# Eight of nine one-hot tiles of the weighted sums made on GpSimd, between the gathers

## The chip, the cores and the metric

The kernel runs on one core of a Trainium2 chip. The core has a matrix engine (TensorE, in the profile PE, with its weight loads PEld), two engines for elementwise work (VectorE or DVE, ScalarE or ACT), GpSimd (POOL), which here issues the indirect transfers that gather rows, and SyncE (SP), which issues the plain transfers. The metric is the device time of one execution in microseconds (us); lower is better.

## The reference

A graph layer over 12500 nodes with 128 features and 412500 edges sorted by destination. For each edge a gate is computed from the difference of the two end nodes, the gated differences are summed per destination, a dense term times the number of incoming edges is added, and the result, with the input added, is normalized per node.

```python
theta = x[dst] - x[src]
w = jax.nn.sigmoid(jax.nn.relu(theta @ W1 + b1) @ W2 + b2)
w_theta = w * theta
agg = jax.ops.segment_sum(w_theta, dst, num_segments=n_nodes)
indeg = jax.ops.segment_sum(jnp.ones((dst.shape[0], 1), x.dtype), dst, num_segments=n_nodes)
out = agg + indeg * (x @ W4 + b4)
x = layernorm(x + out)
```

(Here `n_nodes` is 12500, and the last two lines stand for the return value and the normalization around it.)

## The kernel before, in words

**Tables and edges.** A table `z` in device memory holds for each node 256 values: the 128 products with W1 and the 128 features themselves. The edges, in order of destination, are cut into *parts*. The first 26 parts (`PLAIN`) hold 1024 edges each and serve as a start while tables are built. After them come 234 *later parts* of up to 1656 edges each, numbered s = 26 to 259. Two parts are a block (`b`, `h = divmod(s, 2)`), and a block's results go to a window of 112 nodes (`WB`).

**Two kinds of edges in a later part.** 640 "hot" edges of a later part (`HK`, five tiles of 128) have source nodes that are taken by matrix products from a table kept in SBUF. The others are fetched by eight gathers (`gather`, L369; L380 in the profile), each of 128 rows of 256 values. The gathered tiles k and k+4 hold, row by row, two edges with the same destination, so that four (`J`) one-hot tiles serve all eight. GpSimd's queue holds gather after gather. Between every two stands an instruction that computes nothing that is used: in the later parts a memset of `rest_t`, 128 x 320 (L374). Each is tied by order to the instruction before it, so that the queue is gather, memset, gather, memset. The first gather of a part also waits for the newest TensorE product issued so far (`paced`): that is the pace. The gathers of part s+3 (`LEAD`) are issued in the code of part s.

**Work of a later part** (`part`, L1343), in the order of the code, which is also the order on TensorE, VectorE and ScalarE (their order is written out by hand; GpSimd's follows from the ties just told):
1. `logits`: VectorE subtracts, takes the maximum with zero, multiplies and adds up 1024 columns of gathered rows (L896, L898, L899).
2. `gather(s + 3)` on GpSimd.
3. `add_part(s - 1)`: TensorE sums the part before it (L1083). Each product has a one-hot tile as weights, which says for each of 128 edges to which of the 112 nodes it belongs. There are four one-hot tiles `ow` for the gathered rows and five `owh` for the hot edges, nine in all.
4. gates: `hot_logits` (L1054), `weigh` (L928), `hot_weights` (L1063 and the one-hot tiles `owh`, L1066), `gate_sums`, `one_hot_w` (the one-hot tiles `ow`, L873), the rest of the weighing on ScalarE (L919).
5. `products_ahead`: TensorE's products for the next part (L1025, L1029, L1021, L1040).
6. at the end of a block: its total (L1121, L1129) and normalization (L1156, L1162 and on).
7. `spend`: steps of the placing of the next edge lists (sorting out 64 parts at a time on VectorE: L547, L549, L552, L642 and others), as many as a credit per part allows.

Between steps 2 and 5 ScalarE and TensorE also fetch hot rows (L966, L968, L980).

**The one-hot tiles.** VectorE compares a row of numbers 0 to 111, copied to PSUM (`fix`, `iota_f`), with each edge's place (`rel` for gathered, `hrel` for hot edges, bfloat16). One instruction makes all four `ow` tiles (128 x 448), one makes all five `owh` tiles (128 x 560). They are made in the code of the part itself, and used by `add_part` in the code of the part after it. The buffers of `ow` are four deep and those of `owh` two.

Of the kernel before, what the change touches and what calls it, by code (L numbers as in the profile page):

```python
# [22 lines left out]
K = 8  # L23
# [57 lines left out]
def gnn_resnorm(  # L81
# [284 lines left out]
    table_steps = []  # L366
    paced = {}

    def gather(s):  # L369

        (src_i, _, _), i = set_of(s)
        for k in slots(s):
            if gathers:
                rest = nc.gpsimd.memset(rest_t, 0.0) if s >= NH else nc.gpsimd.engine_nop()  # L374
                tc.add_manual_dep(
                    rest.ins, gathers[-1].ins.name,
                    mybir.DependencyInfo(mybir.DependencyClass.NoSync, mybir.DependencyReason.DATA),
                    reason="between two gathers")
                gathers.append(rest)
# [9 lines left out]
            for other, kind in waits:  # L389
                tc.add_manual_dep(  # L390
                    ins.ins, other.ins.name,
                    mybir.DependencyInfo(kind, mybir.DependencyReason.DATA), reason="gathers' pace")
            gathers.append(ins)


    base_b = const.tile([1, NK], I32, name="base_b")
# [280 lines left out]
    with tc.manual_schedule(engines={SP}), tc.tile_pool(name="work", bufs=2) as wp, tc.tile_pool(  # L677
# [168 lines left out]
        def spread_y(s):  # L846
# [17 lines left out]
                                            y_of(s), start=s >= NH, stop=True, skip_group_check=s < NH)  # L864
            return last

        def one_hot_w(s):

            (_, rel, _), i = set_of(s)
            parts[s]["ow"] = []  # L870
            for k0 in range(0, K if s < PLAIN else J, J):
                ow = wp.tile([P, J, WB], F32, name="ow", bufs=4)
                nc.vector.tensor_tensor(  # L873
                    ow, iota_f.to_broadcast([P, J, WB]),
                    rel[:, k0:k0 + J, i:i + 1].to_broadcast([P, J, WB]), op=OP.is_equal)
                parts[s]["ow"].append(ow)
# [182 lines left out]
        def hot_weights(s):  # L1059

            wx = parts[s]["wxh"]
            for q in range(HQ):
                nc.scalar.activation(wx[:, q, :D], hot_x(s, q), AF.Copy, scale=wx[:, q, D:D + 1])  # L1063
            (_, hrel, _), j = hot_set(s)
            owh = parts[s]["owh"] = wp.tile([P, HQ, WB], F32, name="owh")
            nc.vector.tensor_tensor(  # L1066
                owh, iota_f.to_broadcast([P, HQ, WB]),
                hrel[:, j, :].rearrange("p (q o) -> p q o", o=1).to_broadcast([P, HQ, WB]), op=OP.is_equal)

        def shift(b):  # L1070

# [271 lines left out]
        def part(s):  # L1343
# [26 lines left out]
            if PLAIN + AHEAD <= s + LEAD < NS:  # L1370
                if s >= PLAIN + 4:
                    paced[s + LEAD] = newest[0]
                gather(s + LEAD)
            if PLAIN <= s - 1 < NS:
                add_part(s - 1)
            if now:
# [230 lines left out]
```

## Time and profile before

| | us |
|---|---|
| median of three runs | 3414.64 (3405.97 to 3415.9) |
| the profiled execution, own time | 3395.38 |
| its span | 3393.6 |
| TensorE busy | 2713.4 |
| VectorE busy | 2641.6 |
| ScalarE busy | 2363.5 |
| GpSimd busy | 2821.6 |

The rows quoted below are of four kinds. A *group* row has line, engine, operation, output and inputs, shape and count, then busy us, mean ns of one, and after the second bar the engine's idle us just before these instructions and what ended most of it ("issue" is time in which it waited for nothing that the profile shows). A row *in order of time* has the start and the duration in us, then the instruction; in brackets stands the idle time before it. A row of a *stretch* has its bounds and length, then busy us and count (x) of the instructions asked for or of PE, PEld, DVE, ACT and POOL, then the granted TensorE clock, the DMA share and GB/s. The *chain* gives shares of the span of the work that ended last, followed back from the last instruction.

### The profile page before, as it was taken

To read this page: it belongs to the slowest core of one execution; us is meant where nothing else is said; L and a number is where in the kernel's file an instruction comes from. 1 tells how busy PE (TensorE), PEld (TensorE's weight loads), DVE (VectorE), ACT (ScalarE), POOL (GpSimd) and SP (SyncE) were. 2 spreads that over 40 slices of the span, in tenths; PEclk is the share of its full clock that TensorE was granted. 3 is DMA by queue.
4 is the path that set the end of the run, shared out by engine and by line. 5 is a ranking of instruction groups with operands and counts; after the bars stand their busy time and mean duration, and the time that the engine had idled before them with its cause. 6 is when DMAs were issued, how large, how long until landed. Compare 5 with 4: busy or idle time off the path is not lost.

```text
span 3393.6 us, 62355 instructions
## 1 busy us (share of the span) xinstructions
PE 2713.4 (80%) x18615; PEld 2351.2 (69%) x18615; DVE 2641.6 (78%) x6197; ACT 2363.5 (70%) x5856; POOL 2821.6 (83%) x4093
## 2 busy tenths in 40 slices
PE   6776778787788787888788878888878888888887
PEld 5676767676677676777677766676667777677776
DVE  6797458898888689888888858888887866666666
ACT  4554567776677677777777767777767777777774
POOL 5678778888888888888888888888888888888883
PEclk9876678898899888999898889899988999998998
DMA  7564434444444444444444444444444444444441
GB/s 255 184 169 121 119 93 121 118 111 117 121 113 120 128 113 116 121 117 121 122 118 120 116 118 123 117 117 124 116 115 123 115 122 117 119 122 118 126 110 55
DMA packets 265060, 416.67 MB, mean 123 GB/s; under 512 B 66608, under 2 KB 178217, under 8 KB 264205
## 3 DMA queue, kind: packets, MB, share of 16 engines
q0 software_dynamic: 98528, 267.78, 28.5%
q1 hardware_dynamic: 164219, 138.42, 15.6%
q10 hardware_dynamic: 1970, 6.40, 0.5%
q8 instruction: 154, 2.52, 0.3%
q14 instruction: 189, 1.55, 0.2%
HBM read 384.89 MB, written 27.49 MB: 122 GB/s over the span
## 4 chain that ended last, share of the span: by engine, by line
DVE 30%; ACT 25%; PE 16%; issue 11%; POOL 8%; DMA 5%; another core or an unknown queue 4%; DVEq 0%; SPq 0%; POOLq 0%; ACTq 0%
POOL zbuf L380 6%; ACT wxh L1063 5%; PE pd L980 4%; DVE hh L1054 4%; DVE zbuf L896 4%; DVE zbuf L898 4%; ACT zbuf L919 4%; DVE lg L899 4%; ACT of L966 4%; PE pa L1083 4%; POOL rest_t L374 2%; DMA zbuf<-z,src_i 2%; ACT of L968 2%; DVE ed L549 2%
## 5 line engine op out<-in xcount | busy, mean ns | idle before, releaser
L380 POOL DMA_INDIRECT zbuf<-z,src_i x1866 | 1816.1, 973 | 421.0 <-issue 261.6
L980 PE MATMUL pd<-of,tabs 128*128 128x128 f32 (+4 forms) x4816 | 685.9, 298 | 181.6 <-ACT of L968 95.8
L374 POOL MEMSET rest_t<- 128x320 f32 x2010 | 800.4, 398 | 1.0
L980 PEld LDWEIGHTS pd<-of,tabs 128*128 128x128 f32 x4816 | 628.9, 209 | 224.7 <-ACT of L968 113.5
L1083 PE MATMUL pa<-zbuf,ow 128*112 128x260 f32 (+1 forms) x2282 | 588.1, 406 | 47.6 <-ACT zbuf L919 21.6
L1083 PEld LDWEIGHTS pa<-zbuf,ow 128*112 128x112 f32 x2282 | 407.4, 200 | 157.7 <-ACT zbuf L919 30.1
L1025 PE MATMUL pxa<-wni,xT 128*128 128x128 f32 x1872 | 303.8, 311 | 258.0 <-DVE hh L1054 241.5
L1025 PEld LDWEIGHTS pxa<-wni,xT 128*128 128x128 f32 x1872 | 266.1, 218 | 281.8 <-DVE hh L1054 261.0
L966 ACT ACTIVATE of<-hot_src,nodes 128x512 f32<-128x512 f16 (+3 forms) x602 | 394.1, 709 | 7.1 <-issue 4.3
L919 ACT ACTIVATE zbuf<-zbuf 128x128 f32<-128x128 f32 x1144 | 362.8, 389 | 0.4
L1040 PE MATMUL y<-y,oh 64*128 64x128 f32 x1872 | 341.1, 323 | 14.2 <-issue 14.0
L1029 PE MATMUL pxa<-y,oh 64*128 64x128 f32 x1872 | 336.9, 323 | 9.9 <-issue 9.6
L1054 DVE SCALAR_TENSOR_TENSOR hh<-pxa,w_r 128x128 f32<-128x128 f32 x936 | 270.7, 289 | 92.9 <-remote 48.2
L1083 PEld LDWEIGHTS pa<-wxh,owh 128*112 128x112 f32 x2340 | 295.2, 177 | 34.8 <-issue 12.6
L968 ACT ACTIVATE of<-of 128x1024 f32<-128x1024 f32 (+3 forms) x301 | 310.8, 1033 | 9.2
L1083 PE MATMUL pa<-wxh,owh 128*112 128x130 f32 x2340 | 308.9, 276 | 5.8 <-issue 4.4
L994 ACT ACTIVATE xT<-pd 128x512 f32<-128x512 f32 (+7 forms) x496 | 185.7, 416 | 183.2 <-PE pd L980 59.5
L1029 PEld LDWEIGHTS pxa<-y,oh 64*128 64x128 f32 x1872 | 275.2, 219 | 49.5 <-issue 26.9
L928 DVE TENSOR_TENSOR zbuf<-zbuf,fix 128x512 f32<-128x512 f32 x234 | 160.2, 684 | 186.4 <-ACT fix L903 118.9
L896 DVE TENSOR_TENSOR zbuf<-y,zbuf 128x1024 f32<-128x1024 f32 x234 | 285.5, 1220 | 13.5 <-issue 3.5
L898 DVE SCALAR_TENSOR_TENSOR zbuf<-zbuf,fix 128x1024 f32<-128x1024 f32 x234 | 285.7, 1221 | 8.0
L899 DVE TENSOR_REDUCE lg<-zbuf 128x8 f32<-128x1024 f32 x234 | 285.5, 1220 | 8.0
(265 smaller groups left out, 4710.0 us busy)
## 6 DMA issues: line engine op xcount, KB each, us to landing
to_all<-off_d SPq DMA_DIRECT2D x234, 144.0 KB
hot_src<-hot_s SPq DMA_DIRECT2D x257, 128.0 KB
zbuf<-z,src_i POOLq DMA_INDIRECT x1866
z<-zbuf SPq DMA_DIRECT2D x8, 1024.0 KB
xw<-in_x_dram SPq DMA_DIRECT2D x130, 56.0 KB
u<-u_d SPq DMA_DIRECT2D x130, 56.0 KB
out_dram<-o SPq DMA_DIRECT2D x130, 56.0 KB
y<-z SPq DMA_DIRECT2D x252, 28.0 KB
```

The lines of the kernel that those rows point to most:

```text
L374: rest = nc.gpsimd.memset(rest_t, 0.0) if s >= NH else nc.gpsimd.engine_nop()
L380: ins = nc.gpsimd.indirect_dma_start(out=rows_of(s)[:, k, :], out_offset=None, in_=z if s >= NH else x, in_offset=IndirectOffsetOnAxis(ap= ...
L896: nc.vector.tensor_sub(half, yy.to_broadcast([P, 2, J, D]), half)
L898: nc.vector.scalar_tensor_tensor(h, h, 0.0, w2.to_broadcast([P, K, D]), op0=OP.max, op1=OP.mult)
L899: nc.vector.tensor_reduce(lg[:, :, 0], h, AX.X, OP.add)
L919: nc.scalar.activation(wx[:, k, :D], wx[:, k, :D], AF.Copy, scale=wx[:, k, D:D + 1])
L966: nc.scalar.activation(of[:, t, :], hot_src[:, i % NU, :w], AF.Abs, bias=nodes[:, t:t + 1])
L980: newest[0] = nc.tensor.matmul(to[:, q], tabs[:, g * RG + q, t, :], of[:, t, q], start=t == 0, stop=t == HT - 1)
L1025: nc.tensor.matmul(hot_y(s, q), xT[:, q * P:(q + 1) * P], wneg, start=q % G == 0, stop=False, skip_group_check=True)
L1029: newest[0] = nc.tensor.matmul(hot_y(s, q), d["oh"][:, BP + q * P:BP + (q + 1) * P], y_of(s), start=False, stop=True, skip_group_check=True)
L1054: nc.vector.scalar_tensor_tensor(h, hot_y(s, q), 0.0, w2_r, op0=OP.max, op1=OP.mult, accum_out=lg[:, q, :])
L1083: newest[0] = nc.tensor.matmul(to if len(w.shape) == 3 else to[:, 0, :], one, w, start=first and i == 0, stop=last and i == len(terms) - 1)
```

## The change

The code of later part s now gives `gather(s + 3, ...)` a list of eight small instructions, which make on GpSimd the four `ow` tiles of part s+1 and the first four of its five `owh` tiles. Each is a tensor-scalar comparison of 128 x 112 in SBUF: the row of numbers, in SBUF now (`iota_row`), against one column of places. One of them goes in front of each gather, and the memset between it and the gather has 64 columns instead of 320. VectorE makes only the fifth `owh` tile (128 x 112). The buffers of `owh` become three deep. Parts 28 to 257 have their tiles from GpSimd; parts 26, 27, 258 and 259 have theirs from VectorE as before.

```diff
-    def gather(s):
+    def gather(s, between=()):
         (src_i, _, _), i = set_of(s)
+        between = list(between)
         for k in slots(s):
             if gathers:
-                rest = nc.gpsimd.memset(rest_t, 0.0) if s >= NH else nc.gpsimd.engine_nop()
+                rest = between.pop(0)() if between else None
+                if rest is not None:
+                    tc.add_manual_dep(
+                        rest.ins, gathers[-1].ins.name,
+                        mybir.DependencyInfo(mybir.DependencyClass.NoSync, mybir.DependencyReason.DATA),
+                        reason="between two gathers")
+                    gathers.append(rest)
+                    rest = nc.gpsimd.memset(rest_t[:, :64], 0.0)
+                else:
+                    rest = nc.gpsimd.memset(rest_t, 0.0) if s >= NH else nc.gpsimd.engine_nop()
...
             gathers.append(ins)
+        for fill in between:
+            fill()
...
+        made = {}
+
+        def one_hots_between(s):
+
+            (_, rel, _), i = set_of(s)
+            (_, hrel, _), j = hot_set(s)
+            ow = wp.tile([P, J, WB], F32, name="ow", bufs=4)
+            owh = wp.tile([P, HQ, WB], F32, name="owh", bufs=3)
+            made[s] = ow, owh
+            iota = iota_row[:, :WB]
+
+            def one(to, at):
+                return lambda: nc.gpsimd.tensor_scalar(to, iota, at, None, op0=OP.is_equal)
+
+            return ([one(ow[:, k, :], rel[:, k, i:i + 1]) for k in range(J)]
+                    + [one(owh[:, q, :], hrel[:, j, q:q + 1]) for q in range(K - J)])
+
         def one_hot_w(s):
 
             (_, rel, _), i = set_of(s)
+            if s in made:
+                parts[s]["ow"] = [made[s][0]]
+                return
...
-            owh = parts[s]["owh"] = wp.tile([P, HQ, WB], F32, name="owh")
+            owh, q0 = (made[s][1], K - J) if s in made else (wp.tile([P, HQ, WB], F32, name="owh", bufs=3), 0)
+            parts[s]["owh"] = owh
             nc.vector.tensor_tensor(
-                owh, iota_f.to_broadcast([P, HQ, WB]),
-                hrel[:, j, :].rearrange("p (q o) -> p q o", o=1).to_broadcast([P, HQ, WB]), op=OP.is_equal)
+                owh[:, q0:, :], iota_f.to_broadcast([P, HQ - q0, WB]),
+                hrel[:, j, q0:].rearrange("p (q o) -> p q o", o=1).to_broadcast([P, HQ - q0, WB]),
+                op=OP.is_equal)
...
-                gather(s + LEAD)
+                gather(s + LEAD, one_hots_between(s + 1))
```

## The prediction

> **What bounds the kernel now.** I read the page first (busy times, slices, shares of the chain), then GpSimd's groups of instructions, its order of time, and its stretches.
>
> The page, busy times and the shares of the chain that ended last:
>
> ```profile
> PE 2713.4 (80%) x18615; PEld 2351.2 (69%) x18615; DVE 2641.6 (78%) x6197; ACT 2363.5 (70%) x5856; POOL 2821.6 (83%) x4093
> DVE 30%; ACT 25%; PE 16%; issue 11%; POOL 8%; DMA 5%; another core or an unknown queue 4%; DVEq 0%; SPq 0%; POOLq 0%; ACTq 0%
> ```
>
> By the shares VectorE (DVE) looks like the bound and GpSimd (POOL), at 8%, like a bystander; taking 1 us a part off VectorE then looks like a gain. The groups say otherwise. GpSimd's groups between 600 and 3300 us of the span, a stretch of 2700 us in which only later parts run; then the memset's row by source (min/median/max ns), and three consecutive rows in order of time:
>
> ```profile
> L380 POOL DMA_INDIRECT zbuf<-z,src_i x1711 | 1665.9, 974 | 357.7 <-issue 238.6 <-PE pd L980 29.2 <-remote 23.4
> L374 POOL MEMSET rest_t<- 128x320 f32 x1710 | 680.2, 398 | 0.8
> ...
> L374 POOL MEMSET rest_t<- x1710: 378/379/976, 601.0 to 3299.2; 128x320 f32 x190
> ...
> 1538.38 0.95 POOL L380 DMA_INDIRECT zbuf<-z,src_i  x1 [0.17 <-issue]
> 1539.34 0.38 POOL L374 MEMSET rest_t<- 128x320 f32 x1
> 1539.88 0.95 POOL L380 DMA_INDIRECT zbuf<-z,src_i  x1 [0.17 <-issue]
> ```
>
> A gather, its memset and 0.17 us that precede every gather whatever else happens make 1.50 us. In the 2700 us, 1665.9 + 680.2 + 1711 x 0.17 = 2637 us are this cycle; real waits are the rest of the idle time, 357.7 - 1711 x 0.17 = 66.8 us, 39 ns a gather, 2.5%. GpSimd has practically no spare time. The gathers counted in three stretches show the same:
>
> ```profile
> 600.00:1400.00 800.00, 490.23 (x501) 0.90 0.44 118
> 1400.00:2700.00 1300.00, 803.71 (x823) 0.91 0.45 119
> 2700.00:3300.00 600.00, 371.30 (x388) 0.91 0.44 119
> ```
>
> Eight gathers are a part: 8 x 800/501 = 12.77 us, 8 x 1300/823 = 12.64, 8 x 600/388 = 12.37. Over the same stretches all engines:
>
> ```profile
> 1400.00:2700.00 1300.00, 1054.79 (x7471) 913.47 (x7471) 1086.98 (x2541) 957.65 (x2374) 1131.95 (x1646) 0.91 0.45 119
> 2700.00:3300.00 600.00, 509.64 (x3468) 429.72 (x3468) 381.20 (x930) 439.92 (x1101) 518.68 (x775) 0.91 0.44 119
> ```
>
> VectorE (third figure) falls from 84% to 64% when the placing of edge lists is over, and a part gets only 0.27 us shorter. So relief of VectorE alone has been seen here, and it is worth little. What is left late is a balance: GpSimd waits briefly at the first gather of most parts, for TensorE through the pace:
>
> ```profile
> 2873.57 0.95 POOL L380 DMA_INDIRECT zbuf<-z,src_i  x1 [0.91 <-PE pd L980]
> 2885.77 0.95 POOL L380 DMA_INDIRECT zbuf<-z,src_i  x1 [0.40 <-remote]
> 2898.27 0.95 POOL L380 DMA_INDIRECT zbuf<-z,src_i  x1 [0.69 <-remote]
> ```
>
> So there are two bounds close together: GpSimd's cycle, and the loop through VectorE, ScalarE and TensorE that paces it. What is added to GpSimd's cycle is hidden up to 39 ns a gather, and then costs in full.
>
> **Removed on VectorE.** Its rows, with two others used below:
>
> ```profile
> L873 DVE TENSOR_TENSOR ow<-fix,rel 128x448 f32<-128x448 f32 x286 | 175.4, 614 | 34.6 <-PE pa L1083 17.9 <-remote 16.7
> L1066 DVE TENSOR_TENSOR owh<-fix,hrel 128x560 f32<-128x560 f32 x234 | 171.7, 734 | 0.0
> ...
> L1156 DVE TENSOR_TENSOR own_f<-own_f,a 112x128 f32<-112x128 f32 x130 | 36.1, 277 | 15.7 <-ACT own_f L1138 10.4 <-ACT oh L827 5.1 <-issue 0.2
> L1074 DVE TENSOR_SCALAR sh<-lag,step_c 112x112 f32<-112x112 f32 x12 | 4.0, 354 | 0.0
> ```
>
> One 448-wide tile (614 ns) goes; the 560-wide one shrinks to 112. The two rows give 1.07 ns a column, so 734 - 448 x 1.07 = 255 ns are left. That is 614 + 479 = 1.09 us a part. The parts with gathers number 234; the diff leaves four of them alone (two at the start, two at the end), so 230 x 1.09 = 251 us of VectorE's busy time go. I cost this at nothing in time while GpSimd is the bound. It only removes some of the 39 ns of waiting, which the next paragraphs use up anyway.
>
> **Shorter memset.** How short GpSimd instructions stand at the start of the span (order of time):
>
> ```profile
> 0.25 0.10 POOL L1595 MEMSET const-float32-0.0<- 128x1 f32 x1 [0.25 <-issue]
> 0.75 0.20 POOL masks.py:197 MEMSET wni<- 128x128 f32 x1 [0.29 <-POOLq L1595]
> 0.99 0.23 POOL L247 IOTA iota_row<- 128x128 f32 x1
> 1.19 0.28 POOL masks.py:199 TENSOR_SCALAR_AFFINE_SELECT wni<-wni 128x128 f32<-128x128 f32 x1
> 1.44 0.13 POOL L250 IOTA iota_p<- 128x1 f32 x1
> ```
>
> From 128 columns (200 ns) to 320 (379 ns) is 0.93 ns a column, so 64 columns take 200 - 60 = 140 ns. The mean, 398, is 19 ns over the undisturbed 379; I keep that supplement. The memset saves 239 ns.
>
> **The one-hot on GpSimd** (128x112, compared with a column of scalars, read and written in SBUF). No row shows it. From below: a memset of 112 columns on the same line, 185 ns, since nothing that also reads can be cheaper than writing alone. Nearest row: the affine select, one read and one write, 280 ns at 128 columns, over 100 ns for one column, so 258 ns at 112. The scalar column is extra: on VectorE the operation with one (L1074, 354 ns at 112 columns) takes some 94 ns more than the one without (L1156, 277 at 128, 260 at 112). From above: the 354 ns of VectorE times the ratio of the two engines on a memset of 128 columns (200 against 165 ns, row below), 430 ns. I take the affine select plus half of that scalar price: 258 + 47 = 305 ns, since it is the only row of this engine that reads and writes. Instructions may overlap a little (the select starts 0.20 us after a 0.23 us iota), up to 30 ns; I leave that to the range.
>
> ```profile
> L896 DVE TENSOR_TENSOR zbuf<-y,zbuf 128x1024 f32<-128x1024 f32 x234 | 285.5, 1220 | 13.5 <-issue 3.5 <-remote 3.3 <-DMA zbuf<-z,src_i 2.0
> ...
> L288 DVE MEMSET y<- 128x128 f32 x6 | 0.9, 165 | 0.1
> ```
>
> **New waits.** The one-hot waits for TensorE to be done with its buffer (part s-3 for `ow`, s-2 for `owh`), and behind it stand the gathers of part s+3. Those products are issued before the pace on which the first gather already waits: nothing. TensorE's sums of part s+1 now wait for GpSimd, with the next products behind them:
>
> ```profile
> 1502.93 0.73 DVE L1066 TENSOR_TENSOR owh<-fix,hrel 128x560 f32<-128x560 f32 x1
> 1509.15 1.60 PEld L1083 LDWEIGHTS pa<-zbuf,ow 128*112 128x112 f32 x8
> 1510.59 0.95 POOL L380 DMA_INDIRECT zbuf<-z,src_i  x1 [0.33 <-PE pd L980]
> ```
>
> The sums at 1509.15 are those of the part weighed at 1502.93; a batch of gathers ends just before 1510.59 and would hold the one-hots for the sums due one part later, near 1521. The cover is about 11 us, and L896 waits only 2.0 us in the whole run for gathered rows; without the cover, each us of lag would cost TensorE a us per part. No gather or other DMA moves past another, on GpSimd's queue or on SP's; the gathers come later only by the added time.
>
> **A rule that speaks against it.** Rows first: what stretches GpSimd now is a VectorE tensor-scalar (the memset below takes 0.73), while an operation with two inputs in SBUF (L642) leaves it at 0.38.
>
> ```profile
> 1035.78 1.02 DVE L642 SCALAR_TENSOR_TENSOR et<-ew,ed 128x829 int32<-128x829 int32 x1
> 1036.56 0.38 POOL L374 MEMSET rest_t<- 128x320 f32 x1
> ...
> 1517.37 0.58 DVE L547 TENSOR_SCALAR ew<-ew 128x829 int32<-128x829 int32 x1
> 1517.52 0.73 POOL L374 MEMSET rest_t<- 128x320 f32 x1
> ```
>
> The Trainium skill (SBUF — State Buffer, Who interferes with whom) says that a VectorE instruction with two SBUF inputs contends with a GpSimd instruction that reads SBUF, not with one that only writes. For the memset the trace agrees with it, and no row of this run shows the reading case.
>
> If a GpSimd instruction that reads is held by VectorE's two-input work: the pair around L1156 runs once in two parts; with its successor of similar length it is about 0.6 us, 115 times, so at most 115 x 0.6 = 70 us, and nothing where no one-hot starts inside it. Without such holds the sum below stands; with all, it is 70 us more.
>
> **The sum.** Between two gathers: 305 + 140 + 19 = 464 ns in place of 398, +66 ns. Of the 1866 gathers 1834 get it (229 x 8 + 2; the last part has two): +121 us. Waits that can swallow it: 1834 x 39 ns = 72 us; I let a half go, 36 us, because GpSimd must still wait where TensorE is late, as at 2873.57. Net +85 us. The profiled execution took 3395.4 us (span 3393.6), 0.6% under the median of 3414.64 (three runs, 3405.97 to 3415.9); against its own time the sum is 3480, and on the median's footing 3500 us.
>
> **Rivals.**
> - *Cheap one-hot, faster.* If it runs more like a plain write (185 to 250 ns), the gap is 344 to 409 ns, from 54 ns less to 11 ns more than now, and VectorE's relief may show. At -54 ns the cycle gives 99 us; the pacing loop limits this, as late parts with little VectorE work still take 12.37 us against 12.64 (0.27 x 230 = 62 us). So 3340 to 3400, about 3365. It decides below 305 - 85/1834 = 259 ns for the one-hot, which is where the affine select lies without any price for the scalars: this is close, and speaks for a good chance.
> - *Dear one-hot.* At 430 ns: 430 + 140 + 19 - 398 = +191 ns, x 1834 = 350 us, less 60 us of waits: 3705. For it speaks that the scalar column may be a read of its own on this engine; against it, the 258 ns.
> - *Held by two-input VectorE work* (the pair around L1156): 3500 + 70 = 3570 at most. Against it: the pair is rare.
> - *No change.* A one-hot of 250 to 265 ns: 3405 to 3425.
>
> **How the numbers follow.** A measurement here tells about 0.3% from no change. Forecast (one-hot 265 to 380 ns) 0.47, own range 3425 to 3620; dear 0.14; held 0.06; cheap 0.26; no change 0.07. Slower is 0.67, same 0.07, faster 0.26. The range for 8 in 10 reaches into the cheap case and the dear one: 3350 to 3690.
>
> **What would show it.** GpSimd's row for the one-hot at about 305 ns, x1840; the memset of 64 columns near 140 to 160; GpSimd's real waits down from 39 to some 20 ns a gather, and a part near 13.0 us in all stretches; VectorE busy some 250 us less, its idle time up, most of it put down to gathered rows (L896) or TensorE. The prediction is wrong if the one-hot's row is under 260 ns, or if gathers get shorter or longer than 974 ns beside it.

## The result, and the profile after

| | before | after |
|---|---|---|
| median, us | 3410.3 (3405.25 to 3415.9, four runs) | 4073.75 (4071.84 to 4078.19, four runs) |
| ratio after / before | | 1.1947, 95% interval 1.192 to 1.1973 |
| span of the profiled execution, us | 3393.6 | 4070.0 |
| granted TensorE clock, mean | 0.885 | 0.823 |

The change makes the kernel 19.5% slower. The direction was forecast; the size was not (3500 us, range to 3690). In the changed kernel the gathers are L390, the one-hot tiles L891, the memset of 64 columns L382, TensorE's sums L1117 and the first step on gathered rows L928.

The page of the changed kernel, busy times and the shares of the chain that ended last:

```profile
PE 3014.3 (74%) x18615; PEld 2611.4 (64%) x18615; DVE 2428.0 (60%) x5967; ACT 2383.1 (59%) x5856; POOL 3535.4 (87%) x5933
POOL 46%; PE 17%; ACT 14%; DVE 10%; issue 9%; DMA 3%; another core or an unknown queue 1%; SPq 0%; POOLq 0%; DVEq 0%; ACTq 0%
```

VectorE lost 214 us of busy time, as the edit intends, and GpSimd gained 714 us. Before, GpSimd's share of the chain was 8%, spread among engines that were all nearly the bound. Now it is 46%, by far the largest. GpSimd's queue looks like what sets the time; the first experiment tests it.

GpSimd's groups of the changed kernel between 600 and 3300 us, shapes kept apart:

```profile
L390 POOL DMA_INDIRECT zbuf<-z,src_i x1370 | 1446.6, 1056 | 233.5 <-issue 196.0 <-ACT zbuf L951 9.7 <-ACT wxh L1095 7.1
L891 POOL TENSOR_SCALAR owh<-iota_row,hrel 128x112 f32<-128x112 f32 x684 | 419.4, 613 | 23.7
L891 POOL TENSOR_SCALAR ow<-iota_row,rel 128x112 f32<-128x112 f32 x686 | 418.9, 611 | 23.9
L382 POOL MEMSET rest_t<- 128x64 f32 x1370 | 221.0, 161 | 0.0
```

Two rows differ from the forecast. A one-hot tile takes 612 ns, not 305. A gather takes 1056 ns, not 974. The memset, 161 ns, is as forecast (140 plus 19). In the same 2700 us stood 1711 gathers before, 1370 now, so the mean distance from gather to gather went from 2700/1711 = 1.578 to 2700/1370 = 1.971 us. The difference of 0.393 us, times the 1834 gathers that get the change, is 721 us. From the first to the last of the 1866 gathers (386.9 to 3344.4 us before, 391.6 to 4042.3 after) it is 693 us, as the difference is smaller outside this window. The spans differ by 676 us, because behind the last gather's start the changed kernel has 28 us left where the kernel before has 49.

Busy time and count of the gathers in the three stretches of the changed kernel:

```profile
600.00:1400.00 800.00, 429.06 (x405) 0.83 0.35 95
1400.00:2700.00 1300.00, 694.99 (x660) 0.83 0.36 95
2700.00:3300.00 600.00, 322.04 (x305) 0.83 0.36 95
```

A part is 8 x 800/405 = 15.8 us, then 15.8, then 15.7. Before, the parts grew shorter towards the end (12.77, 12.64, 12.37). Now they are the same whatever VectorE has to do: the sign of one queue that runs without a pause. The group row says so too: 233.5 us of idle time before 1370 gathers is the 0.17 us that stand before each (1370 x 0.17 = 232.9), and no real wait is left.

One cycle of that queue in order of time (changed kernel, GpSimd only):

```profile
1502.14 1.03 POOL L390 DMA_INDIRECT zbuf<-z,src_i  x1 [0.16 <-issue]
1503.21 0.58 POOL L891 TENSOR_SCALAR ow<-iota_row,rel 128x112 f32<-128x112 f32 x1
1503.73 0.16 POOL L382 MEMSET rest_t<- 128x64 f32 x1
1504.06 1.03 POOL L390 DMA_INDIRECT zbuf<-z,src_i  x1 [0.17 <-issue]
```

Gather to gather is 1504.06 - 1502.14 = 1.92 us against 1.50 before. The gather itself is 0.08 longer (1.03 against 0.95). From its end to the next one's start it is 0.89 against 0.55: the one-hot tile starts 0.04 behind the gather, the memset starts 0.52 behind the one-hot's start, takes 0.16, and then come the 0.17 that stand before every gather. Note the order: the memset starts at 1503.73, before the one-hot's shown end of 1503.79. So 1834 x (0.34 + 0.08) = 770 us, less at most the 72 us of waits counted before, gives 3395 + 698 = 4093 us, 0.5% over the measured 4073.75.

The waits of the changed kernel (total us, times, longest us):

```profile
PEld pa L1117 <- POOL owh L891: 1044.3, 718, 2.9
PE pa L1117 <- POOL owh L891: 867.6, 660, 2.7
DVE zbuf L928 <- DMA zbuf<-z,src_i: 428.3, 128, 7.9
```

TensorE now waits 868 us for one-hot tiles, and VectorE 428 us for gathered rows, where it waited 2.0 before. Both queues wait for GpSimd. Read by itself, the first row looks like a cause. The first experiment shows that it isn't one.

### The profile page after: what moved, and what is told of

It reads as the page before. It is cut to its first block, busy times and chain, and to the rows that moved or that the text cites. A ratio compares the mean times of both kernels' runs of the same rounds, so it can differ in the third digit from the quotient of the medians.

```text
span 4070.0 us, 64414 instructions
## 1 busy us (share of the span) xinstructions
PE 3014.3 (74%) x18615; PEld 2611.4 (64%) x18615; DVE 2428.0 (60%) x5967; ACT 2383.1 (59%) x5856; POOL 3535.4 (87%) x5933
## 4 chain that ended last, share of the span: by engine, by line
POOL 46%; PE 17%; ACT 14%; DVE 10%; issue 9%; DMA 3%; another core or an unknown queue 1%; SPq 0%; POOLq 0%; DVEq 0%; ACTq 0%
POOL zbuf L390 28%; POOL owh L891 9%; POOL ow L891 7%; PE pd L1012 7%; PE pa L1117 4%; POOL rest_t L382 2%; ACT of L998 2%; ACT wxh L1095 2%; ACT zbuf L951 2%; DMA zbuf<-z,src_i 2%; DVE hh L1086 2%; ACT of L1000 1%; PE pxa L1057 1%; DVE zbuf L930 1%; DVE zbuf L928 1%
## 5 line engine op out<-in xcount | busy, mean ns | idle before, releaser
L390 POOL DMA_INDIRECT zbuf<-z,src_i x1866 | 1959.1, 1050 | 333.0 <-issue 267.1
L1117 PE MATMUL pa<-wxh,owh 128*112 128x130 f32 x2340 | 566.0, 357 | 869.0 <-POOL owh L891 867.6
L1117 PEld LDWEIGHTS pa<-wxh,owh 128*112 128x112 f32 x2340 | 385.8, 215 | 1055.5 <-POOL owh L891 1044.3
L1012 PE MATMUL pd<-of,tabs 128*128 128x128 f32 (+4 forms) x4816 | 916.7, 370 | 32.3 <-ACT of L1000 30.7
L1012 PEld LDWEIGHTS pd<-of,tabs 128*128 128x128 f32 x4816 | 893.1, 285 | 42.8 <-ACT of L1000 32.8
L891 POOL TENSOR_SCALAR owh<-iota_row,hrel 128x112 f32<-128x112 f32 x920 | 559.7, 608 | 31.7
L891 POOL TENSOR_SCALAR ow<-iota_row,rel 128x112 f32<-128x112 f32 x920 | 557.5, 606 | 32.0
L1117 PE MATMUL pa<-zbuf,ow 128*112 128x260 f32 (+1 forms) x2282 | 551.6, 388 | 44.1 <-ACT zbuf L951 28.1
L928 DVE TENSOR_TENSOR zbuf<-y,zbuf 128x1024 f32<-128x1024 f32 x234 | 285.9, 1222 | 436.3 <-DMA zbuf<-z,src_i 428.3
L1117 PEld LDWEIGHTS pa<-zbuf,ow 128*112 128x112 f32 x2282 | 385.3, 190 | 136.2 <-ACT zbuf L951 30.4
L1163 DVE TENSOR_TENSOR a<-a,pa 112x130 f32<-112x130 f32 x117 | 34.1, 292 | 563.4 <-ACT a L1155 420.7
L382 POOL MEMSET rest_t<- 128x64 f32 x1834 | 296.3, 162 | 0.0
```

The source lines that it names most:

```text
L382: rest = nc.gpsimd.memset(rest_t[:, :64], 0.0)
L390: ins = nc.gpsimd.indirect_dma_start(out=rows_of(s)[:, k, :], out_offset=None, in_=z if s >= NH else x, in_offset=IndirectOffsetOnAxis(ap= ...
L891: return lambda: nc.gpsimd.tensor_scalar(to, iota, at, None, op0=OP.is_equal)
L928: nc.vector.tensor_sub(half, yy.to_broadcast([P, 2, J, D]), half)
L1012: newest[0] = nc.tensor.matmul(to[:, q], tabs[:, g * RG + q, t, :], of[:, t, q], start=t == 0, stop=t == HT - 1)
L1117: newest[0] = nc.tensor.matmul(to if len(w.shape) == 3 else to[:, 0, :], one, w, start=first and i == 0, stop=last and i == len(terms) - 1)
```

## The experiments

Theory after the result: *price*. The one-hot tile on GpSimd costs some 0.34 us of queue time per gather more than what it replaces, the gather behind it 0.08 more, and nothing else matters. Rivals: *late tiles* (TensorE's waits for the tiles make the loss or part of it), *relief* (VectorE's lost work gives something back), *short rest* (the memset of 64 columns lengthens the gathers or disturbs something). The runs were made on three chips, called A (e1 to e4; before 3361.28 us), B (e5 to e8; before 3305.11) and C (e9 to e15; before 3305 to 3307). On which chip the first comparison ran (before 3410.3) is not known, and the changed kernel was not run again on A, B or C; where its time is set beside an experiment's, that is across chips. Diffs are cut; they are against the changed kernel where no other is named.

### e1: the price alone

VectorE makes all nine tiles as before; GpSimd makes eight too, into tiles that nobody reads.

```diff
+        spare_ow = const.tile([P, J, WB], F32, name="sow"), const.tile([P, J, WB], F32, name="sowh")
...
-            ow = wp.tile([P, J, WB], F32, name="ow", bufs=4)
-            owh = wp.tile([P, HQ, WB], F32, name="owh", bufs=3)
-            made[s] = ow, owh
+            ow, owh = spare_ow
```

> VectorE makes all nine tiles as before; GpSimd makes eight more into a scratch tile that nobody reads, with the 64-column memset behind each. If GpSimd's cycle alone sets the time (1.92 us a gather in the changed kernel against 1.50), this is as slow as the changed kernel: 4040 to 4110 us, with TensorE no longer waiting for GpSimd's tiles but VectorE for gathered rows instead. If the cost came from TensorE waiting for late tiles (868 us of its idle time), it is clearly faster than the changed kernel, 3450 to 3800 us.

4071.72 us, ratio 1.2116 (1.209 to 1.2141): the time of the changed kernel, 4073.75, to 0.05%. GpSimd's gathers in e1 and half of its eight tiles a part; then the gathers in the changed kernel:

```profile
L390 POOL DMA_INDIRECT zbuf<-z,src_i x1866 | 1959.9, 1050 | 325.1 <-issue 252.1
L890 POOL TENSOR_SCALAR sow<-iota_row,rel 128x112 f32<-128x112 f32 x920 | 548.2, 596 | 31.8
L390 POOL DMA_INDIRECT zbuf<-z,src_i x1866 | 1959.1, 1050 | 333.0 <-issue 267.1 <-ACT of L1000 15.1 <-ACT zbuf L951 14.9
```

And e1's longest waits of VectorE and TensorE (total us, times, longest us):

```profile
DVE zbuf L927 <- DMA zbuf<-z,src_i: 937.1, 208, 9.2
PE pxa L1056 <- DVE hh L1085: 931.8, 209, 9.3
```

No tile of GpSimd's is waited for here, and the time is the same. VectorE waits 937 us for rows, where the changed kernel shows 428 us: the same slack, seen at another place. By the times alone, the cost of *late tiles* and the gain of *relief* could cancel, since e1 takes both away. The idle time before the gathers excludes it: 325.1 us here and 333.0 in the changed kernel are hardly more than 1866 x 0.17 = 317 us, so in neither does GpSimd wait for anything that TensorE or VectorE could give it sooner. So *late tiles* falls as a cost, and *relief* is worth nothing once GpSimd is the bound.

### e2: the relief alone

GpSimd makes nothing, the memset stays 320 wide, and TensorE reads a constant tile in place of the eight that VectorE no longer makes, so that the sums are not the reference's.

```diff
-            made[s] = ow, owh
+            made[s] = owc, None
+            return ()
...
-            terms += [(d["owh"][:, q, :], d["wxh"][:, q, :]) for q in range(HQ)]
+            terms += [(owc[:, q, :] if s in made and q < J else d["owh"][:, q, :], d["wxh"][:, q, :]) for q in range(HQ)]
```

> VectorE is relieved exactly as in the change, GpSimd does what it did before: the eight tiles are read from one constant tile (the sums are then not the reference's). If GpSimd's cycle was the bound before, the gain is at most its real waits, 72 us: 3340 to 3410 us. If VectorE was the bound, most of its 251 us come out: 3150 to 3250 us.

3337.47 us, ratio 0.9932 (0.9911 to 0.9953). The page's busy row:

```profile
PE 2687.1 (81%) x18615; PEld 2344.5 (70%) x18615; DVE 2416.4 (73%) x5971; ACT 2361.0 (71%) x5856; POOL 2827.7 (85%) x4093
```

Some 225 us of VectorE's busy time (2641.6 to 2416.4) buy 24 us, 0.7%.

### e3: the short memset alone, on chip A

Against the kernel before:

```diff
-                rest = nc.gpsimd.memset(rest_t, 0.0) if s >= NH else nc.gpsimd.engine_nop()
+                rest = nc.gpsimd.memset(rest_t[:, :64] if s >= PLAIN + AHEAD else rest_t, 0.0) if s >= NH else nc.gpsimd.engine_nop()
```

> The kernel before, with only the memset between the gathers of later parts cut from 320 to 64 columns, 239 ns less a gather. If GpSimd's cycle was the bound, the time falls until the pacing loop takes over, by 20 to 150 us: 3260 to 3390 us, and GpSimd waits some 200 ns a gather for the pace. If the pacing loop was the bound, or the rest is needed for something, no gain or a loss: 3400 to 3500 us. The length of the gathers (952 ns median before, 1030 in the changed kernel) tells whether the short memset is what lengthens them.

3802.53 us, ratio 1.131 (1.1286 to 1.1335). This fits no theory: GpSimd has 0.22 us less to do per gather, and the kernel is 13% slower. Its gathers are not lengthened (982 ns), so a short rest is not what makes them 1056 in the changed kernel. GpSimd's group of gathers in e3:

```profile
L380 POOL DMA_INDIRECT zbuf<-z,src_i x1866 | 1832.8, 982 | 1221.2 <-PE last L1029 471.1 <-PE pd L980 430.0 <-issue 254.2
```

TensorE in order of time in e3:

```profile
1516.44 0.27 PE L1029 MATMUL pxa<-y,oh 64*128 64x128 f32 x1
1517.01 0.27 PE L1040 MATMUL y<-y,oh 64*128 64x128 f32 x1 [0.30 <-issue]
1517.04 0.47 PE L1029 MATMUL pxa<-y,oh 64*128 64x128 f32 x2
1517.74 0.27 PE L1040 MATMUL y<-y,oh 64*128 64x128 f32 x1 [0.23 <-issue]
1518.47 0.27 PE L1040 MATMUL y<-y,oh 64*128 64x128 f32 x1 [0.47 <-issue]
1519.20 0.42 PE L1021 MATMUL pxb<-wni,xT 128*128 128x128 f32 x2 [0.46 <-issue]
```

Just before these rows the products of each of the two lines (L1029, L1040) follow each other every 0.11 us. From 1517.01 on one comes every 0.73 us (1517.01, 1517.74, 1518.47, 1519.20), and the idle time before it has no releaser ("issue"). The granted clock is 1.00 in both stretches of 2 us from 1516 to 1520, so it isn't a lowered clock that spaces them. GpSimd then waits for TensorE at the pace: 471 + 430 us. Summed over TensorE's rows of waits, this idle time without a releaser was 553 us in 694 places. The last experiment comes back to it.

### e4: prices on GpSimd, side by side

The eight instructions of a part are replaced by eight different ones, each with the memset of 64 behind it, output unused.

```diff
+                lambda: g.tensor_scalar(a[0], iota, col, None, op0=OP.is_equal),
+                lambda: g.tensor_scalar(a[1][:, :16], iota[:, :16], col, None, op0=OP.is_equal),
+                lambda: g.tensor_scalar(a[2], iota, 5.0, None, op0=OP.is_equal),
+                lambda: g.tensor_scalar(a[3], iota, iota_p, None, op0=OP.is_equal),
+                lambda: g.tensor_copy(a[4], iota),
+                lambda: g.tensor_scalar(a[5], iota, 5.0, None, op0=OP.add),
+                lambda: g.tensor_scalar(owh[:, 2:4, :], iota.rearrange("p (o m) -> p o m", o=1).to_broadcast([P, 2, WB]), col, None, op0=OP.is_equal),
+                lambda: g.memset(a[7], 0.0),
```

> As e1, but the eight scratch instructions of a part differ: comparison with a bfloat16 column at 112, 16 and 224 columns of output, with a constant at 112, with a float32 column at 112, copy at 112, addition of a constant at 112, memset at 112. If the column of scalars is what makes the one-hot 588 ns long, the constant form takes 260 to 350 ns and 16 columns still over 400. If it is the price per column, 16 columns take under 200 ns and the constant form stays near 590. If it is the comparison, the addition is cheaper than the comparison with a constant.

GpSimd's groups (sixth to eighth row: a comparison with a constant, a copy, a memset; the one before them adds a constant):

```profile
L902 POOL TENSOR_SCALAR sowh<-iota_row,rel 128x224 f32<-128x224 f32 x230 | 233.7, 1016 | 7.4
L896 POOL TENSOR_SCALAR sow<-iota_row,rel 128x112 f32<-128x112 f32 x230 | 138.6, 603 | 7.8
L899 POOL TENSOR_SCALAR sow<-iota_row,iota_p 128x112 f32<-128x112 f32 x230 | 138.6, 602 | 6.0
L897 POOL TENSOR_SCALAR sow<-iota_row,rel 128x16 f32<-128x16 f32 x230 | 82.1, 357 | 7.9
L901 POOL TENSOR_SCALAR sowh<-iota_row 128x112 f32<-128x112 f32 x230 | 120.8, 525 | 16.1
L898 POOL TENSOR_SCALAR sow<-iota_row 128x112 f32<-128x112 f32 x230 | 115.4, 502 | 16.1
L900 POOL COPY sowh<-iota_row 128x112 f32<-128x112 f32 x230 | 67.2, 292 | 1.3
L903 POOL MEMSET sowh<- 128x112 f32 x230 | 51.1, 222 | 0.2
```

The time of this kernel, one run, was 3898.99 us. From 16 to 112 columns the comparison grows by 246 ns, 2.6 ns a column; what is left at no columns is 0.32 us. The 224 columns lie on the same line by their median, 882 ns; their mean of 1016 is raised by some long ones. The price is thus both a fixed part and a part per column, and neither was foreseen at this size. It is not the column of places: a column in float32 costs the same (602), and with a constant in its place the row shows 100 ns less but the distance from the gather's end to the next gather's start, counted in order of time, stays (0.93 us at the median against 0.89). It is not the comparison either: adding a constant gives 525 and 0.94. A copy of the same size, which also reads and writes, takes less than half (292; distance 0.56), a memset 222 (0.46). The costly thing is the tensor-scalar instruction as such.

### e5: what a gather sees of the work around it

The eight gaps of a part get different contents, the output unused. The time, one run, was 3711.06 us.

```diff
+            return [[short], [long], [hot[0]], [hot[1], long], [hot[2], short],
+                    [lambda: g.tensor_copy(owh[:, 0, :], iota), short], [hot[3], one(owh[:, 1, :], rel[:, 3, i:i + 1]), short], [g.engine_nop]]
```

> As e1 (scratch tiles), but what stands in front of the eight gathers of a part differs: memset of 64; memset of 320; one-hot alone; one-hot and memset of 320; one-hot and memset of 64; copy of 112 and memset of 64; two one-hots and memset of 64; an empty instruction. If a tensor-scalar since the last gather is what lengthens a gather from 952 to 1030 ns, then the third, fourth, fifth and seventh gather have 1030 and the others 950 to 980. If the short distance from the one-hot's writes does it, the fourth has 950. If the one-hot's price is its own, the second of two in a row adds 0.50 us and more; if half of it comes from following a gather, it adds under 0.35 us.

GpSimd in order of time, two gathers behind a memset and two behind a one-hot tile:

```profile
1506.02 0.95 POOL L384 DMA_INDIRECT zbuf<-z,src_i  x1 [0.16 <-issue]
1506.97 0.38 POOL L886 MEMSET rest_t<- 128x320 f32 x1
1507.52 0.95 POOL L384 DMA_INDIRECT zbuf<-z,src_i  x1 [0.17 <-issue]
1508.50 0.58 POOL L882 TENSOR_SCALAR sow<-iota_row,rel 128x112 f32<-128x112 f32 x1
1509.26 1.03 POOL L384 DMA_INDIRECT zbuf<-z,src_i  x1 [0.17 <-issue]
1510.32 0.59 POOL L882 TENSOR_SCALAR sow<-iota_row,rel 128x112 f32<-128x112 f32 x1
1510.85 0.37 POOL L886 MEMSET rest_t<- 128x320 f32 x1
1511.38 1.03 POOL L384 DMA_INDIRECT zbuf<-z,src_i  x1 [0.17 <-issue]
```

The medians over the whole run, from a gather's end to the next one's start and then that next gather's length (us):

| between two gathers | distance | next gather |
|---|---|---|
| empty instruction | 0.31 | 0.95 |
| memset 64 | 0.33 | 0.95 |
| memset 320 | 0.55 | 0.95 |
| copy + memset 64 | 0.56 | 0.99 |
| one-hot | 0.79 | 1.03 |
| one-hot + memset 64 | 0.89 | 1.03 |
| one-hot + memset 320 | 1.10 | 1.03 |
| two one-hots + memset 64 | 1.42 | 1.03 |

A second one-hot adds 0.53 us, and so does the start-to-start distance: 0.53 is what it occupies of the queue. A gather whose gap holds a tensor-scalar is 80 ns longer, once, whether a memset stands between or not, and two don't add more. Why is open.

### e6 to e8: three changes of size, on chip B

e6, the kernel before with a memset of 448 columns:

```diff
-    rest_t = const.tile([P, 320], F32, name="rest_t")
+    rest_t = const.tile([P, 448], F32, name="rest_t")
...
-                rest = nc.gpsimd.memset(rest_t, 0.0) if s >= NH else nc.gpsimd.engine_nop()
+                rest = nc.gpsimd.memset(rest_t if s >= PLAIN + AHEAD else rest_t[:, :320], 0.0) if s >= NH else nc.gpsimd.engine_nop()
```

> The kernel before with a memset of 448 columns instead of 320 in the later parts: 0.93 x 128 = 119 ns more a gather, no tensor-scalar anywhere. If GpSimd's cycle sets the time as soon as its waits of 39 ns are used up: 1834 x (119 - 39 to 119) = 147 to 218 us more, 3505 to 3580 us. If gathers themselves or tiles are needed for a loss, no loss: 3350 to 3380 us.

3473.59 us, ratio 1.0505 (1.0485 to 1.0525), +168 us. The increase is within the expected 147 to 218 us; the time is under the expected one, which was counted from chip A's 3361, and so is that of e7. GpSimd's group:

```profile
L374 POOL MEMSET rest_t<- 128x448 f32 x1834 | 919.5, 501 | 1.0
```

(501 - 398) ns x 1834 = 189 us are added, 168 arrive. Work that is nothing but time on GpSimd costs nearly its full length. Only 21 us are swallowed.

e7, only the four `ow` tiles on GpSimd:

```diff
-            made[s] = ow, owh
+            made[s] = ow, None
...
-            return ([one(ow[:, k, :], rel[:, k, i:i + 1]) for k in range(J)]
-                    + [one(owh[:, q, :], hrel[:, j, q:q + 1]) for q in range(K - J)])
+            return [one(ow[:, k, :], rel[:, k, i:i + 1]) for k in range(J)]
...
+            owh, q0 = wp.tile([P, HQ, WB], F32, name="owh"), 0
```

> The change for the four ow tiles alone, in front of the first four gathers of a part; VectorE makes the five owh tiles, and the other four gathers keep the memset of 320. If the price is 0.42 us for each gather with a one-hot, less the waits: 230 x 4 x 0.42 - 72 to 0 = 314 to 386 us more, 3675 to 3750 us. If the cost of the change came from the late owh tiles at the end of the list, it is near the kernel before, 3340 to 3420 us.

3669.38 us, ratio 1.1095 (1.1073 to 1.1116), +364 us: about 917 gaps at 0.42 us are 385, less what is swallowed. The loss goes roughly by the number of tiles.

e8, the changed kernel without the memset behind a one-hot tile:

```diff
                 if rest is not None:
-                    tc.add_manual_dep(
...
-                    rest = nc.gpsimd.memset(rest_t[:, :64], 0.0)
+                    pass
```

> The change without the memset of 64 behind each one-hot. If that memset is only its own 0.16 us: 4072 - 1834 x 0.16 = 3780 us (3740 to 3830), still slower than the kernel before. If the gather lengthens in its place, near 4000 us.

3867.72 us, ratio 1.1697 (1.1672 to 1.1723). It saves 206 us of the changed kernel's 4073.75 and is some 40 us above the top of what was expected. Of the 206 us, 25 lie before the first later gather (at 391.6 us in the changed kernel, 366.3 here), where the edit changes nothing. From the first to the last later gather it is 3650.7 us against 3473.0, which is 178 us or 97 ns a gather, and not the 160 ns of the memset's row. The table of e5 says why: without the memset the distance is 0.79, with it 0.89. It starts before the one-hot's end and adds only some 0.1.

### e9 to e15: how long should the rest be? On chip C

e9, e11 and e12 are the kernel before with memsets of 256, 192 and 128 columns (the edit of e3 with that number); e10 puts six memsets of 320 ahead of a part's first gather and 64 columns ahead of the other seven:

```diff
+                for w in ([320] * 6 if k == 0 else [64]) if s >= PLAIN + AHEAD else [320]:
...
```

> The kernel before with a memset of 256 columns instead of 320, 60 ns less a gather. If what made e3 13% slower sets in as soon as GpSimd no longer holds TensorE back, this is slower too, by 1 to 6%; if only a much shorter rest does it, the cycle's 60 ns show as far as the pacing loop allows, 0 to 2% faster.

> The kernel before with memsets of 64 columns in front of seven of a part's gathers and six memsets of 320 in front of the first, so that GpSimd's time for a part is about as before (within 0.3 us of 12.0 us) while its gathers stand closer together. If e3 was slow because TensorE ran ahead and was then granted a lower clock, GpSimd's cycle holds it back here and the time is within 2% of the kernel before, with the clock at 0.87 or above. If it was slow because gathers close together disturb the loads or the other engines, this is slower by 8 to 15% as well, with the clock near 0.82.

> The kernel before with a memset of 192 columns, 119 ns less a gather. Between 256 columns (1.5% faster) and 64 (13% slower). If TensorE is throttled as soon as GpSimd's cycle leaves it more room than its other work needs, the clock falls below 0.88 and the time is 2 to 10% above the kernel before; if the loss sets in only with much room, 1 to 3% faster, with the clock at 0.89 or above.

> The kernel before with a memset of 128 columns, 179 ns less a gather. By the first reading 6 to 13% slower, clock near 0.82; by the second between 2% faster and 5% slower.

| memset columns | us | ratio to before | 95% interval |
|---|---|---|---|
| 256 (e9) | 3254.89 | 0.9846 | 0.983 to 0.9863 |
| 192 (e11) | 3227.89 | 0.9778 | 0.9755 to 0.9802 |
| 128 (e12) | 3195.64 | 0.968 | 0.9657 to 0.9704 |
| bunched (e10) | 3464.8 | 1.048 | 1.0463 to 1.0498 |

Each step gains; e12 gained more than either of its two readings had allowed. From 320 to 128 columns the memset's mean falls from 398 to 229 ns, 310 us in all, and 109 us arrive; GpSimd's idle time before its gathers grows by 188 us (345.6 in e15, 533.8 in e12). The cycle of GpSimd is a bound, and a second one lies not far under it. The bunched run is slower because its block of six took longer than planned:

```profile
1512.12 2.90 POOL L375 MEMSET rest_t<- 128x320 f32 x6
```

GpSimd's cycle over eight gathers came to 13.16 us (1581 gathers in 2600 us), where the kernel before has 12.5 on this chip (835 gathers in 1300 us, e15). 0.7 us for some 230 parts is 160 us, and 158 were lost. By the medians from start to start, seven short gaps and the long one are 7 x 1.28 + 3.84 = 12.8 us, where 12.0 were planned. So the run had a slower cycle and says nothing about bunching by itself.

With e3 this leaves a contradiction: 128 columns gain 3.2%, 64 columns lose 13%. Either there is a threshold between them, or it is the chip. So both ran side by side on chip C (e13 is the kernel of e3, e14 that of e12), with the kernel before, unchanged, profiled beside them (e15).

> The kernel before with a memset of 64 columns between two gathers, a second time, beside one of 128 columns on the same chip. Theory 'length': a rest as short as 64 columns is itself what makes TensorE stutter; then this run is 8 to 14% slower than before, with some 500 us of TensorE idle time put down to issue. Theory 'chip': the stutter belongs to the chip that the first run of it had (there TensorE's idle time put down to issue was 26, 106, 553 and 40 us in the four kernels; in the eight kernels on two other chips it was 9 to 11 us in each). Then, on a chip with about 10 us of it, this run is 3 to 5% faster than before; on a chip with the stutter it is slower, and so is the run with 128 columns.

> The kernel before with a memset of 128 columns, beside the one of 64 on the same chip. Theory 'length': 2.5 to 4% faster than before on every chip, with about 10 us of TensorE idle time put down to issue. Theory 'chip': 2.5 to 4% faster where the kernel before shows about 10 us of such idle time, and slower by some per cent, with hundreds of us of it, where the kernel before shows 100 us or more.

> The kernel before, unchanged, for its trace on the chip of the two runs beside it. TensorE's idle time put down to issue says which kind of chip it is: about 10 us where it takes some 3305 us, 100 to 200 us where it takes 3360 to 3410 us. If the time goes with the chip but not with this idle time, theory 'chip' has no ground.

64 columns: 3171.15 us, ratio 0.9595 (0.9571 to 0.962). 128 columns: 3198.28, ratio 0.9672 (0.965 to 0.9693). The kernel before: 3305.71. The same kernel that lost 13% on chip A gains 4% on chip C, so the length of the rest alone is not the cause. Two groups of e13, GpSimd's gathers and TensorE's line that stuttered in e3:

```profile
L380 POOL DMA_INDIRECT zbuf<-z,src_i x1866 | 1829.4, 980 | 603.6 <-issue 227.8 <-PE pd L980 171.1 <-PE last L1029 124.6
...
L1040 PE MATMUL y<-y,oh 64*128 64x128 f32 x1872 | 323.5, 323 | 0.0
```

The same line in e3, and in the trace of before that the prediction read:

```profile
L1040 PE MATMUL y<-y,oh 64*128 64x128 f32 x1872 | 329.2, 300 | 119.1 <-issue 118.1
```

```profile
L1040 PE MATMUL y<-y,oh 64*128 64x128 f32 x1872 | 341.1, 323 | 14.2 <-issue 14.0
```

TensorE's idle time without a releaser, summed over its rows of waits: 7.8 us in e15, 8.1 in e13, 9 to 11 in every other run on chips B and C; on chip A 553 us in e3, 106 in e2, 26 and 40 in e1 and e4. In the first comparison it is 193 us in the trace of before that the prediction read, and 17 in that of the changed kernel. That the stutter doesn't come from the length of the rest alone is shown by e3 against e13, the same kernel on A (3798.8 to 3805.06 us in four executions) and on C (3163.14 to 3180.0). That it is the chip, and not something else that differed between the two occasions, rests on one chip each. What it is stays open: nothing in the traces names it. The transfers of instructions are the same in both (queue q8: 154 packets, 2.52 MB). On chip A the stutter is small where GpSimd's queue is the bound (26 and 40 us, against 106 and 553). It would fit that the kernel before takes 3305, 3361 or 3410 us, while GpSimd's price alone (e1) and the changed kernel take 4072 and 4074 beside 3361 and 3410; that was not tested by itself.

So the fastest version found is the kernel before with a short memset, 64 columns on chip C. On chip A that same kernel loses 13%, and 128 columns weren't tried there.

## Why the prediction was right and wrong

**What bounds the kernel: right, and it gave the direction.** GpSimd's cycle with little to spare, hidden behind an 8% share of the chain, was the right reading. e6 shows it from one side (189 us added, 168 arrive) and e9, e11, e12 from the other. The slack of 39 ns a gather was in part, it seems, the chip's: the trace read for it has 421.0 us of idle time before the gathers, of which the stutter may be a part; on chip C (e15) the same row has 345.6.

**Removed on VectorE: right.** Costed at nothing, and worth nothing: e1 keeps all of VectorE's work and takes the same time. By itself (e2) it is worth 0.7%. The busy time fell by 214 us rather than 251; of 230 x (614 + 734 - 268) = 248 us that were removed by the rows (the one `owh` tile left takes 268 ns), some 34 came back as longer rows of VectorE elsewhere; why was not looked into.

**Shorter memset: right by its row, wrong in the sum.** 161 ns mean against 159. But behind a one-hot it adds only 0.10 us to the distance (e5, e8), since it starts before the one-hot ends.

**The one-hot on GpSimd: the term that failed.** Predicted 305 ns, with 185 and 430 as ends; measured 588 at the median, 606 to 613 in the mean, and 0.53 us from start to start. Even by the last, most lenient figure it is beyond the upper end. Both ways of bounding it were unsound. The affine select (258 ns scaled) was taken as a stand-in for any instruction that reads and writes; e4's copy (292) would fit that, its tensor-scalar doesn't. The upper end took VectorE's price times the ratio of the two engines' memsets, 200/165; for a tensor-scalar of 112 columns the ratio is 603/354 = 1.7. The supplement for the scalar column, 47 ns, was for something that costs nothing in the queue (e4).

**Gathers unchanged: wrong.** The prediction named a gather other than 974 ns as what would refute it, but put the change at nothing, without a row that shows a gather behind such an instruction. Measured: +82 ns in the window (974 to 1056), times 1834 = 150 us, almost a quarter of the loss.

The sum redone with measured terms: distance 0.89 - 0.55 = +0.34 us, gather +0.08, times 1834 = 770 us. With those two terms and the prediction's own 36 us of waits it would have said 3395 + 734 = 4129, 1.4% over the result, or 4149 counted, like its 3500, from the median before. The mechanism was right; two sizes were off: the one-hot's term of 305 ns (with the memset, 66 ns more a gap instead of the measured 340) and the gather's term of nothing (80 ns).

**New waits: right in their effect, wrong in their cover.** The cover of some 11 us is gone: TensorE waits 868 us for the tiles. It costs nothing, since e1 has no such wait and the same time, and GpSimd hardly waits for TensorE in either.

**A rule that speaks against it: the row is now there.** The prediction had no row for a GpSimd instruction that reads beside VectorE work with two inputs. The changed kernel has one, in order of time:

```profile
1243.08 1.06 DVE L654 SCALAR_TENSOR_TENSOR ew<-ed,et 128x829 int32<-128x829 int32 x1
1243.20 1.37 POOL L891 TENSOR_SCALAR owh<-iota_row,hrel 128x112 f32<-128x112 f32 x1
```

1.37 us against 0.58 alone: it is held until the VectorE instruction is nearly through. The Trainium skill (SBUF — State Buffer, Who interferes with whom) says that such pairs contend when GpSimd reads; this row agrees. But the mean of the one-hots lies only 24 ns over their median, 24 x 1840 = 44 us at most, other holds included. The bound of 70 us in the prediction holds, but not by its reason. It was made for the pair around L1156 alone, and the row above is a step of the placing. Of all 1840 one-hots 98 are longer than 0.70 us, together 33 us over the median; 19 of them overlap most with L1196, the second of that pair, and 50 with L559, a VectorE tensor-scalar with one tensor input (L547 before, beside which the memset took 0.73).

**Rivals.** *Held* is answered above, and *no change* needed a one-hot of 265 ns at most. *Dear one-hot* was the right kind of case, and with 3705 us far too low. *Cheap one-hot* needed 259 ns; it was off by a factor of two, and its 0.26 was not earned by any row of a tensor-scalar on GpSimd. Its limit, "the pacing loop", was wrong as well: the late parts of 12.37 us were mostly GpSimd's own cycle (8 x 1.50 = 12.0), not a loop that cannot go faster. In e13 a stretch of 400 us after 2700 us holds 310 gathers, 10.3 us a part:

```profile
2700.00:3100.00 400.00, 294.89 (x310) 0.97 0.54 144
```

**The range: too low.** Its upper end, 3690, rested on 430 ns as an upper bound for an operation of which the trace had no row on this engine.

## What to carry to other kernels

An operation that moves to another engine needs a price from that engine and that kind of instruction; a memset or a select there, or the same operation elsewhere times a ratio, was off by two and bounded nothing. Where an engine's queue is full, count start to start, and count the neighbours too: here the instruction behind was 80 ns longer. And idle time without a releaser can be absent from the same kernel on another chip: see there before it is counted as slack or an edit is blamed for it.

## What the runs showed of the hardware that was not expected

- On GpSimd a tensor-scalar instruction costs some 0.32 us plus 2.6 ns a column (357 ns at 16, 603 at 112), while a copy of 112 columns takes 292 ns. With a constant for the column of scalars, or an addition for the comparison, the row is shorter (502, 525), but the next gather comes no sooner (0.93 and 0.94 us behind the one before, against 0.89).
- A gather takes 0.95 us behind a memset, 0.99 behind a copy and 1.03 behind a tensor-scalar (e5). It stays open why.
- The granted TensorE clock falls as gaps grow, from a mean of 0.885 to 0.823, here without showing in the time, since GpSimd hardly waits (333.0 us before 1866 gathers, 317 of them the 0.17 us each). All engines (PE, PEld, DVE, ACT, POOL), then the clock, in stretches of 2 us of the changed kernel:

```profile
1510.00:1512.00 2.00, 0.55 (x3) 0.27 (x2) 0.00 (x0) 2.00 (x9) 1.80 (x4) 1.00 0.28 80
...
1514.00:1516.00 2.00, 0.66 (x3) 0.66 (x4) 0.00 (x0) 0.00 (x0) 1.80 (x4) 0.50 0.24 72
1516.00:1518.00 2.00, 2.00 (x11) 2.00 (x11) 0.67 (x3) 0.59 (x3) 1.80 (x4) 0.50 0.22 66
...
1520.00:1522.00 2.00, 2.00 (x20) 1.88 (x21) 1.94 (x3) 1.57 (x4) 1.80 (x4) 0.84 0.21 61
1522.00:1524.00 2.00, 2.00 (x21) 1.64 (x19) 1.93 (x3) 1.43 (x3) 1.80 (x4) 1.00 0.24 70
```

  After some 4 us of little TensorE work (from 1510) the clock is at 0.50; work resumes at 1516, and within the stretch from 1520 the clock comes back, 4 to 6 us later. At 0.50 a full stretch holds 11 products, at 1.00 it holds 21. The Trainium skill (TensorE: Matmul & The Clock Gate, Part 1: The HAM clock gate) describes a clock that idle time halves and sustained work restores, each after some 3.4 us; the trace agrees in kind, and its times here look somewhat longer.
- The stutter of TensorE on one chip, a product every 0.73 us with no releaser (e3), against none of it in the same kernel on another (e13), goes with 3802.53 - 3171.15 = 631 us, nearly as much as the change itself costs (663). Some 55 of the 631 also separate the kernel before on the two chips.
